# Layer 2 between images: the k, v and output projections by seven products of half-size blocks, with the block sums on VectorE

## Chip, cores and metric

The kernel runs on one core of one Trainium2 chip. The metric is device time in microseconds (us) of one execution, inputs laid out and output stored in the chip's memory. The core has five engines with an instruction queue each: TensorE (PE: matrix products, with a separate row PEld for loading the stationary operand), VectorE (DVE), ScalarE (ACT), GpSimd (POOL) and SyncE (SP, which here only issues transfers). Each executes its own queue in order; they meet at semaphores.

## The reference

Four layers on x of shape (4, 512, 32, 32) in float32: four images of 512 channels and 1024 tokens. Each layer normalizes x by groups of channels (`_gn`) and adds what it computes to x. Layer 0 is an attention with heads mixed, layer 1 a gate per channel, layer 3 a lookup of the eight best of 2048 memory rows. Layer 2 is what the change touches: a plain attention with 8 heads of 64 channels.

```python
def _L2_conv_ref(x, Wq, bq, Wkv, bkv, Wp, bp):        # x: _gn(x), shape (b, 512, 32, 32)
    q = _conv1x1(x, Wq, bq)
    k, v = jnp.split(_conv1x1(x, Wkv, bkv), 2, axis=1)
    ...                                               # to (b, 8, 64, 1024)
    attn = jax.nn.softmax(jnp.einsum('bhct,bhcs->bhts', q, k) * SCALE, axis=-1)
    out = jnp.einsum('bhts,bhcs->bhct', attn, v)
    return _conv1x1(out.reshape(b, c, h, w), Wp, bp)  # _conv1x1: 512 x 512 weights times 512 x 1024
x = x + _L2_conv_ref(_gn(x), ...)
```

Each of the four projections of an image is a product of a 512 x 512 matrix with a 512 x 1024 one.

## The kernel before

Everything is float32. Channels lie on the 128 partitions, in `KC` = 4 chunks; tokens run along the free dimension, cut in two halves of `NB` = 512. [...]

Layer 2 works on the images one after the other (`for b in range(B)`). For image b, 16 units of attention come first (`scores2`, `apply2`): four score tiles per unit, their exponentials on ScalarE, sums of pairs of exponentials on GpSimd and VectorE, and the products with v. Then, for b = 0, 1 and 2, comes the stretch between images, on TensorE in this order: `take_q2` (q of image b+1), the last `apply2` of b, `take_k2` with the denominators' product `rs` of b in it (`invert2`), `take_v2`, the first four score tiles of b+1, and `put_out2` (output projection of b). The last image is followed by `put_out2` alone. q, k and the output go through `project` (L192), v through `project_tokens` (L204); a projection is 32 products of 128 x 128 with 128 x 512, in four groups of eight, and each group fills a PSUM tile of two banks, `sc`, of which the pool `ps_s` has three. The score tiles and the small products of the normalizations (`small_ps`) take tiles of the same pool. A group is evacuated at once: q on VectorE (L989), k on ScalarE with its bias (L996), v on VectorE with its bias (L1005), and the output as two additions of 512 columns on VectorE (L1136) to a row block `xr_c` that ScalarE has scaled (L1134), followed by `bn_stats` (L1138).

`invert2` takes the denominators on a way through memory: `rs` on TensorE, a copy on ScalarE (L1099), a reciprocal on VectorE (L1100), a store `r` and a load `rb` by SP (L1106, L1109). `finish2` (L1121, VectorE) multiplies with `rb` and writes the attention's result `o`.

Beside the units run two chains of small steps as Python generators: `behind` (normalization for layer 3, `norm3`, and the gate of layer 1 for the last images, `gating`) and `ahead` (`prepare2`: normalized input `xn` of the next image). The loop takes a step of `behind` twice in each unit from the third on. All inner instructions keep the order in which they are written (`pin`); what isn't pinned is placed by the scheduler. Weights are loaded anew for each image into three rotating buffers (`eight_k`). The memory matrix of layer 3, `memT`, is loaded before layer 2 begins.

Of the kernel before, what the change touches and what calls it, by code (L numbers as in the profile page):

```python
# [10 lines left out]
F32 = mybir.dt.float32  # L11
AF = mybir.ActivationFunctionType
ALU = mybir.AluOpType
# [3 lines left out]
P = 128  # L17
B = 4
C = 512
T = 1024  # L20
KC = C // P
TC = T // P
NB = 512
# [6 lines left out]
NI = 2048  # L30
# [11 lines left out]
def fast_net(ctx: ExitStack, tc: tile.TileContext, a: dict, out: bass.AP, flag: bass.AP):  # L42
    nc = tc.nc
# [12 lines left out]
    def pin(ins):  # L56

        return tc.keep_in_program_order(ins)
# [182 lines left out]
    def big(tag, name):  # L241

        return apool.tile([P, KC, T], F32, tag=tag, name=name)
# [43 lines left out]
    def run_out(gen):  # L287
        for _ in gen:
            pass
# [662 lines left out]
    def prepare2(b, in_steps=False):  # L952

        I = img[b]
        mv2, s1, t1 = l2[b]
        if not in_steps:
            yield
        gm, rstd, _ = yield from coeffs(mv2[:, 0, :], mv2[:, 1, :], f"c{b}")
        sa = small.tile([P, KC], F32, tag="sa", name=f"sa_{b}")
        ta = small.tile([P, KC], F32, tag="ta", name=f"ta_{b}")  # L960
        nc.gpsimd.tensor_mul(sa, s1, rstd)
        nc.gpsimd.tensor_sub(ta, t1, gm)
        nc.gpsimd.tensor_mul(ta, ta, rstd)
        tb = I["tb"] = small.tile([P, KC], F32, tag="tb", name=f"tb_{b}")
        nc.gpsimd.tensor_add(tb, t1, bp2)
        if in_steps:
            yield from normalized(b, sa, ta)
            return
        xn = I["xn"] = big("xn", f"xn_c{b}")
        for k in range(KC):  # L970
            nc.sync.dma_start(out=xn[:, k, :], in_=x1[b][:, k, :])
        yield
        yield
        for k in range(KC):
            pin(nc.vector.tensor_scalar(
                xn[:, k, :], xn[:, k, :], sa[:, k:k + 1], ta[:, k:k + 1],
                ALU.mult, ALU.add,
            ))
            yield

    def load2(b):
        for key in ("Wq", "Wk", "Wv"):
            img[b][key] = load_w(key, f"{key}2_{b}")

    def take_q2(b, m, at=None):
        I = img[b]
        if m == 0:
            I["q"] = big("q", f"q2_{b}")
        project(I["Wq"], tokens(I["xn"]), m, at, lambda ps: pin(nc.vector.tensor_scalar(  # L989
            I["q"][:, m, :], ps, bq2[:, m:m + 1], SCALE, ALU.add, ALU.mult)), f"q2_{b}")  # L990

    def take_k2(b, m, at=None):
        I = img[b]
        if m == 0:
            I["k"] = big("k", f"k2_{b}")
        project(I["Wk"], tokens(I["xn"]), m, at, lambda ps: pin(nc.scalar.activation(  # L996
            I["k"][:, m, :], ps, AF.Identity, bias=bk2[:, m:m + 1])), f"k2_{b}")

    def take_v2(b, i, at=None):
        I = img[b]  # L1000
        if i == 0:
            I["v"] = big("v", f"v2_{b}").rearrange("p k (i c) -> p (k i) c", c=C)
        project_tokens(
            I["Wv"], lambda k, t: I["xn"][:, k, t * P:(t + 1) * P], i, at,
            lambda ps: pin(nc.vector.tensor_add(  # L1005
                I["v"][:, 2 * i:2 * i + 2, :], ps,
                bv2.rearrange("p c -> p () c").to_broadcast([P, 2, C]))), f"v2_{b}")
# [148 lines left out]
    def prepare3(b):  # L1156
        xn = xn3[b] = (o_full.rearrange("p (k t) -> p k t", k=KC) if b % 2
                       else big("xn", f"xn_d{b}"))
        gc3 = l3[b][1]
        for k in range(KC):  # L1160
            nc.sync.dma_start(out=xn[:, k, :], in_=x2[b][:, k, :])
        yield
        for k in range(KC):
            pin(nc.scalar.activation(
                xn[:, k, :], xn[:, k, :], AF.Identity,
                bias=gc3[:, 0, k:k + 1], scale=gc3[:, 1, k:k + 1],
            ))
            yield

    def attention(b, tt, between=None):  # L1170

        nm = f"{b}_{tt}"
        att = eight_k([P, NI], f"att_{nm}")
        for i, (lo, hi) in enumerate(
                ((0, T), (T, T + NB), (T + NB, NI)) if (b, tt) == tiles[-1] else ((0, T), (T, NI))):
            sc = ps_s.tile([P, T], F32, tag="sc", name=f"at_{nm}_{i}")
            for i0 in range(lo, hi, NB):
                for k in range(KC):
                    pin(nc.tensor.matmul(  # L1179
                        sc[:, i0 - lo:i0 - lo + NB],  # L1180
                        xn3[b][:, k, tt * P:(tt + 1) * P], memT[k][:, i0:i0 + NB],
                        start=(k == 0), stop=(k == KC - 1),
                    ))
# [261 lines left out]
    sums2 = eT_flat[:, 6 * 2 * NB:8 * 2 * NB].rearrange("p (i r q) -> p i r q", i=2, r=2)  # L1445
    pair_sum = e.rearrange("p i r qq k -> p i r (qq k)")
    memT = []
    for k in range(KC):
        if k < 2:
            m_ = apool.tile([P, NI], F32, tag="s2", bufs=2, name=f"memT{k}")  # L1450
        else:
            m_ = eT_flat[:, (4 + k) * NI:(5 + k) * NI]
        nc.sync.dma_start(out=m_, in_=a["memT"][k * P:(k + 1) * P, :])
        memT.append(m_)
# [4 lines left out]
    for b in range(B):  # L1459
        last = b + 1 == B  # L1460
        behind = chain(
            behind if b else state["behind"], norm3(b - 1) if b > 0 else gating(B - 1))
        ahead = prepare3(0) if last else prepare2(b + 1)
        for s, u in enumerate(UNITS2):
            if s == 5 and not last:
                load2(b + 1)
            if s == 5 and last:
                img[b]["Wp"] = load_w("Wp", f"Wp2_{b}")
            if s >= 1:
                scores2(b, u, UNITS2[s - 1])  # L1470
            for _ in range(2):
                if s >= 3:
# [4 lines left out]
        if not last:  # L1477
            for m in range(KC):
                take_q2(b + 1, m)
            img[b]["Wp"] = load_w("Wp", f"Wp2_{b}")  # L1480
        apply2(b, UNITS2[-1])
        if not last:
            for m in range(KC):
                take_k2(b + 1, m)
                if m == 0:
                    invert2(b)
        if last:
            atts[0] = attention(*tiles[0], lambda: invert2(b))
        finish2(b)
        if not last:  # L1490
            for i in range(TC // 2):
                take_v2(b + 1, i)
            scores2(b + 1, UNITS2[0])
        put_out2(b)

    def check_range():

# [751 lines left out]
```

## Time and profile before

| | |
|---|---|
| median of 3 runs | 2588.38 us (2588.32 to 2590.48) |
| the profiled execution's own time | 2587.3 us |
| its span, first to last instruction | 2585.5 us |
| TensorE clock granted over the span | 0.999 |
| busy share: PE, PEld, DVE, ACT, POOL | 98%, 45%, 60%, 38%, 46% |
| layer 2's stretch after image 0 on the chain that ended last | 1392.48 (q) to 1510.59 (end of the output projection) us |

The profile comes from one execution. Its page gives the busy time of each engine, the span in 40 slices, the chain of work that ended last (followed back from the last instruction), and groups of instructions by line, with busy time, the mean duration of one and the idle time of the engine ahead of them. Records of TensorE overlap, so its cost per record is the time of a run of records divided by their number, not the mean duration. Lines such as L192 are those of the kernel before.

### The profile page before, as it was taken

What the parts mean: (1) busy time and instruction counts of PE and PEld (TensorE: products, weight loads), DVE (VectorE), ACT (ScalarE), POOL (GpSimd) and SP (SyncE); (2) the same over time, 40 slices, a digit from 0 to 9 for tenths busy, and PEclk for the clock granted to TensorE, in tenths of its full rate; (3) what the DMA queues carried; (4) which work ended last, traced back from release to release, by engine and by line L of the source; (5) the groups of instructions that cost most, each with busy time, mean ns of one, the idle gap of its engine ahead of it and who ended that gap; (6) DMA issues with size and microseconds to landing.
All of it is one profiled execution on the core that took longest, in us unless ns stands there. A gap on an engine that the chain in (4) does not pass through costs nothing.

```text
span 2585.5 us, 47491 instructions
## 1 busy us (share of the span) xinstructions
PE 2533.4 (98%) x18438; PEld 1162.9 (45%) x18438; DVE 1548.0 (60%) x2668; ACT 986.9 (38%) x1165; POOL 1199.9 (46%) x1700
## 2 busy tenths in 40 slices
PE   8999999999999999999999999999999999999998
PEld 3344535544355534555533433443343344444445
DVE  4599348872788338881466047225614647878876
ACT  1467236651666236651252145125304622121211
POOL 3266415543455425553284047017404616656565
PEclk9999999999999999999999999999999999999999
DMA  2578448872698439883300120030012036667666
GB/s 82 144 208 233 124 125 228 232 205 82 180 239 235 113 95 224 236 254 122 130 18 15 68 101 21 25 137 27 13 42 97 22 110 184 216 185 219 180 192 180
DMA packets 186969, 358.22 MB, mean 139 GB/s; under 512 B 32873, under 2 KB 96361, under 8 KB 183026
## 3 DMA queue, kind: packets, MB, share of 16 engines
q1 hardware_dynamic: 105504, 175.57, 21.9%
q0 software_dynamic: 49152, 142.79, 20.1%
q10 hardware_dynamic: 32082, 36.76, 5.1%
q8 instruction: 148, 2.42, 0.4%
q14 instruction: 83, 0.68, 0.1%
HBM read 186.96 MB, written 33.82 MB: 85 GB/s over the span
## 4 chain that ended last, share of the span: by engine, by line
PE 74%; issue 8%; POOL 7%; DMA 7%; ACT 2%; DVE 1%; SPq 0%; POOLq 0%; ACTq 0%; DVEq 0%
PE pair L192 10%; PE sc_c L1027 9%; PE pv_c L1064 9%; PE pv L532 8%; POOL got L1204 7%; PE pair L467 6%; PE pair L493 5%; PE pt L425 4%; PE pt L721 4%; PE p L192 3%; PE k L192 3%; PE q L192 3%; PE v L204 3%; DMA got<-in_mem,ix 3%; DMA s<-ss 3%
## 5 line engine op out<-in xcount | busy, mean ns | idle before, releaser
L482 POOL DMA_DIRECT2D s<-ss x512 | 258.2, 511 | 399.1 <-ACT ss L473 103.3
L506 DVE STREAM_TRANSPOSE eT<-e 128x1024 f32<-128x1024 f32 x256 | 316.8, 1238 | 195.4 <-ACT e L500 194.9
L1204 POOL DMA_INDIRECT got<-in_mem,ix x256 | 277.6, 1085 | 216.2 <-DVE tmx L1210 144.3
L1021 ACT ACTIVATE eT<-sc_c 128x1024 f32<-128x1024 f32 x256 | 247.9, 1022 | 289.2 <-PE sc_c L1027 210.4
L521 DVE BATCH_NORM_STATS2 st<-e 128x6 f32<-128x256 f32 x1024 | 351.1, 406 | 0.0
L500 ACT ACTIVATE e<-pair 128x1024 f32<-128x1024 f32 x256 | 250.4, 1022 | 168.7 <-PE pair L493 139.0
L1045 POOL TENSOR_TENSOR e<-eT 128x1024 f32<-128x1024 f32 x96 | 235.6, 2457 | 161.6 <-ACT eT L1021 100.5
L467 PE MATMUL pair<-k,q 64*32 64x512 f32 x4096 | 267.1, 598 | 12.7 <-ACT e L500 12.7
L473 ACT COPY ss<-pair 128x1024 f32<-128x1024 f32 x256 | 247.2, 1020 | 78.6 <-PE pair L467 37.5
L532 PE MATMUL pv<-eT,v 128*64 128x128 f32 x4096 | 250.7, 276 | 8.9 <-ACT pv L592 8.9
L532 PEld LDWEIGHTS pv<-eT,v 128*64 128x64 f32 x4096 | 221.1, 137 | 76.7 <-issue 54.5
L1046 DVE TENSOR_TENSOR eT<-eT,e 128x1024 f32<-128x1024 f32 x96 | 138.7, 1444 | 179.0 <-POOL e L1045 178.9
L1027 PE MATMUL sc_c<-q,k 64*128 64x512 f32 x1024 | 237.2, 602 | 2.4 <-DVE xr L684 2.3
L1064 PE MATMUL pv_c<-eT,v 128*64 128x512 f32 x1024 | 234.7, 601 | 1.6 <-DVE eT L1121 1.6
L1041 POOL TENSOR_TENSOR eT<-eT 128x1024 f32<-128x1024 f32 x32 | 80.0, 2500 | 335.8 <-ACT eT L1021 332.0
L493 PE MATMUL pair<-s,wmix 32*32 32x512 f32 x4096 | 161.8, 599 | 3.1 <-DMA s<-ss 1.9
L1251 DVE SCALAR_TENSOR_TENSOR acc<-got,et,acc 128x512 f32<-128x512 f32 x210 | 157.9, 752 | 7.5
L1027 PEld LDWEIGHTS sc_c<-q,k 64*128 64x128 f32 x1024 | 93.5, 186 | 131.7 <-issue 72.0
L1184 ACT COPY att<-at 128x1024 f32<-128x1024 f32 (+1 forms) x65 | 64.9, 999 | 220.9 <-PE at L1179 220.8
L467 PEld LDWEIGHTS pair<-k,q 64*32 64x32 f32 x4096 | 57.1, 105 | 179.6 <-ACT e L500 86.3
L1064 PEld LDWEIGHTS pv_c<-eT,v 128*64 128x64 f32 x1024 | 68.4, 138 | 139.9 <-issue 138.1
L1179 PE MATMUL at<-memT,xn_d 128*128 128x512 f32 x256 | 120.7, 594 | 0.0
(295 smaller groups left out, 3299.4 us busy)
## 6 DMA issues: line engine op xcount, KB each, us to landing
s<-ss SPq DMA_DIRECT2D x512, 128.0 KB
s<-ss POOLq DMA_DIRECT2D x512, 128.0 KB, 4.6
rb<-r POOLq DMA_DIRECT2D x64, 128.0 KB, 6.1
o<-o SPq DMA_DIRECT2D x32, 256.0 KB
xr<-in_x ACTq DMA_DIRECT2D x32, 256.0 KB
x<-xr SPq DMA_DIRECT2D x32, 256.0 KB
xr_c<-x SPq DMA_DIRECT2D x32, 256.0 KB
rb_c<-r SPq DMA_DIRECT2D x64, 128.0 KB
```

What stands on the lines that cost most here:

```text
L192: pin(nc.tensor.matmul(ps[:, n, :], w[:, k, m * P:(m + 1) * P], rhs(k, n), start=(k == 0), stop=(k == KC - 1),))
L467: pin(nc.tensor.matmul(sc[m * NS:(m + 1) * NS, r, :], q[r * HD:(r + 1) * HD, m, s * NS:(s + 1) * NS], k_[r * HD:(r + 1) * HD, m, n * NB:(n ...
L482: pin(relays[side].dma_start(out=s2[2 * m + r::NH], in_=ss[m * NS:(m + 1) * NS, r, :]))
L493: pin(nc.tensor.matmul(mixed(s, r // 2)[t * NS:(t + 1) * NS, r % 2, :].rearrange("p (qq k) -> p qq k", qq=2), wmix[r * NS:(r + 1) * NS], s ...
L500: pin(nc.scalar.activation(e[:, half].rearrange("p r qq k -> p (r qq k)"), flat2(mixed(s, half)), AF.Exp))
L506: pin(nc.vector.transpose(eT[:, j % 2].rearrange("p b (qq i r) x -> p i r qq b x", qq=2, i=4)[:, i, 2 * half:2 * half + 2], e[:, half].rea ...
L521: pin(nc.vector.bn_stats(st[:, i, 2 * half + r, qq, :], e[:, half, r, qq, :]))
L532: pin(nc.tensor.matmul(pv[r * HD:(r + 1) * HD, gp, :], I["v"][:, t, g * HD:(g + 1) * HD], eT[:, j % 2, t, :, 4 * g:4 * g + 4], start=(t == ...
L1021: pin(nc.scalar.activation(e, scs[len(es)], AF.Exp))
L1027: pin(nc.tensor.matmul(sc[:, r, :], I["k"][r * HD:(r + 1) * HD, m, t * P:(t + 1) * P], I["q"][r * HD:(r + 1) * HD, m, n * NB:(n + 1) * NB] ...
L1064: pin(nc.tensor.matmul(pv[r * HD:(r + 1) * HD, :], I["v"][:, t, h * HD:(h + 1) * HD], e[:, r, :], start=(t == 0), stop=(t == TC - 1),))
L1204: pin(nc.gpsimd.indirect_dma_start(out=got[:, i, :], out_offset=None, in_=a["mem"], in_offset=bass.IndirectOffsetOnAxis(ap=ix[:, i:i + 1], ...
```

## The change

For b = 0, 1 and 2 the k, v and output projections are computed by seven products of half-size blocks (256 x 256 blocks of the weights with 256 x 512 blocks of the input) in place of eight. Each of the seven is four products of 128 x 128 with 128 x 512 (k and output, `by_channels`) or eight of 128 x 128 with 128 x 256 (v, `by_tokens`), accumulated in pairs, and takes one `sc` tile. The sums of blocks that the products need are made on VectorE: of the input in `input_sums` (five additions of 128 x 1024 for k and v together, five for the output), of each weight matrix once, in `weight_sums` (five additions of 128 x 512, between image 0 and 1); the summed weights are stored to memory (`w_sums`) and loaded in place of the plain ones afterwards. Each of the seven results goes into one or two of the four blocks of the projection: the first use of a block is written by `begin` (ScalarE for k and output, VectorE for v), the others are added or subtracted in place by VectorE. The output's blocks are finished by `done`: a `scalar_tensor_tensor` with the row block, `bn_stats`, and a store of the whole block.

It also moves things. The steps of `behind` leave the units (but for the last image) and are taken between the groups of q, the products of k and those of v. `memT` is loaded at the beginning of the last image, since the block sums lie in its place. The last image keeps `put_out2`.

```diff
     def load2(b):
         for key in ("Wq", "Wk", "Wv"):
-            img[b][key] = load_w(key, f"{key}2_{b}")
+            load_sums(b, key, b == 1 or key == "Wq")
...
+    def input_sums(src):
+        b11, b12, b21, b22 = quarters(src, NB)
+        t1, t3, t4 = places7["in"]
+        return ((lambda: add7(t1, b11, b22), lambda: sub7(t4, b21, b11), lambda: sub7(t3, b12, b22)),
+                (lambda: add7(b21, b21, b22), lambda: add7(b12, b11, b12)))
...
+    SEVEN = (
+        (1, ((0, 0, "="), (1, 1, "="))),
+        (4, ((0, 0, "+"), (1, 0, "="))),
+        (3, ((0, 1, "="), (1, 1, "+"))),
+        (5, ((0, 0, "-"), (0, 1, "+"))),
+        (2, ((1, 0, "+"), (1, 1, "-"))),
+        (7, ((0, 0, "+"),)),
+        (6, ((1, 1, "+"),)),
+    )
+    LAST7 = {3: (5, (0, 1)), 4: (2, (1, 0)), 5: (7, (0, 0)), 6: (6, (1, 1))}
...
+    def seven(b, key, src, multiply, view, block, begin, done=None):
...
+        for i, (at, uses) in enumerate(SEVEN):
+            ps = ps_s.tile([P, 2, NB], F32, tag="sc", name=f"{key}_{b}_{at}")
+            multiply(ps, *factors[at])
+            for *ij, op in uses:
+                if op == "=":
+                    begin(*ij, ps)
+                else:
+                    (add7 if op == "+" else sub7)(block(*ij), block(*ij), view(ps))
+            if done and i in LAST7:
+                done(*LAST7[i][1])
+            yield
+
+    def by_channels(ps, w, x):
+        for m in range(2):
+            for k in range(2):
+                pin(nc.tensor.matmul(
+                    ps[:, m, :], w[:, k, m * P:(m + 1) * P], x[:, k, :],
+                    start=(k == 0), stop=(k == 1)))
+
+    def by_tokens(ps, w, x):
+        for t in range(4):
+            for k in range(2):
+                pin(nc.tensor.matmul(
+                    by_head(ps)[:, t, :], x[:, k, t * P:(t + 1) * P], w[:, k, :],
+                    start=(k == 0), stop=(k == 1)))
...
+        def done(i, j):
+            for m in range(2 * i, 2 * i + 2):
+                part = dst[:, m, j * NB:(j + 1) * NB]
+                pin(nc.vector.scalar_tensor_tensor(
+                    part, rows.pop((m, j)), s1[:, m:m + 1], part, ALU.mult, ALU.add))
+                pin(nc.vector.bn_stats(st[m][:, j, :], part))
...
-            for m in range(KC):
-                take_k2(b + 1, m)
-                if m == 0:
-                    invert2(b)
+        for i, _ in enumerate(seven_k(b + 1)):
+            if i == 0:
+                invert2(b)
+                for fn in later:
+                    fn()
+            if i == 4 and b == 0:
+                weight_sums(0, "Wp")
+            next(behind, None)
         finish2(b)
...
-            for i in range(TC // 2):
-                take_v2(b + 1, i)
-            scores2(b + 1, UNITS2[0])
-        put_out2(b)
+        early, later = input_sums(img[b]["o"])
+        for i, _ in enumerate(seven_v(b + 1)):
+            if 2 <= i < 5:
+                early[i - 2]()
+            elif i >= 5:
+                later[i - 5]()
+            next(behind, None)
+        run_out(behind)
+        scores2(b + 1, UNITS2[0])
+        seven_out(b)
```

More of the change, by code (lines that the diff above doesn't have):

```diff
@@ L982, in load2, with load_sums @@
         for key in ("Wq", "Wk", "Wv"):
-            img[b][key] = load_w(key, f"{key}2_{b}")
+            load_sums(b, key, b == 1 or key == "Wq")
+    def load_sums(b, key, plain):
+        w = img[b][key] = eight_k([P, KC, C], f"{key}2_{b}")
+        nc.sync.dma_start(out=w, in_=a[key] if plain else w_sums[key])
+    H = C // 2
+    w_sums = {key: dram.tile([P, KC, C], F32, tag=f"ws_{key}", name=f"ws_{key}")
+              for key in ("Wk", "Wv", "Wp")}
+    places7 = {}
+    add7, sub7 = (lambda *t: pin(nc.vector.tensor_add(*t))), (lambda *t: pin(nc.vector.tensor_sub(*t)))
@@ new lines, in quarters, with weight_sums @@
+    def quarters(t, step):
+        return [t[:, 2 * h:2 * h + 2, i * step:(i + 1) * step]
+                for h in range(2) for i in range(2)]
+    def input_sums(src):
[3 more added lines that the diff above has]
+                (lambda: add7(b21, b21, b22), lambda: add7(b12, b11, b12)))
+    def weight_sums(b, key):
+        w = img[b][key]
+        a11, a21, a12, a22 = quarters(w, H)
+        s1, s6, s7 = places7[key]
+        add7(s1, a11, a22)
+        sub7(s7, a12, a22)
+        add7(a12, a11, a12)
+        sub7(s6, a21, a11)
+        add7(a21, a21, a22)
+        nc.sync.dma_start(out=w_sums[key], in_=w)
@@ new lines, in fast_net, with by_head @@
+    SEVEN = (
[8 more added lines that the diff above has]
+    LAST7 = {3: (5, (0, 1)), 4: (2, (1, 0)), 5: (7, (0, 0)), 6: (6, (1, 1))}
+    def by_head(ps):
+        return ps.rearrange("p n (t c) -> p (n t) c", c=H)
+    def seven(b, key, src, multiply, view, block, begin, done=None):
+        a11, s2, s5, a22 = quarters(img[b][key], H)
+        s1, s6, s7 = places7[key]
+        b11, t6, t7, b22 = quarters(src, NB)
+        t1, t3, t4 = places7["in"]
+        factors = {1: (s1, t1), 2: (s2, b11), 3: (a11, t3), 4: (a22, t4),
+                   5: (s5, b22), 6: (s6, t6), 7: (s7, t7)}
+        for i, (at, uses) in enumerate(SEVEN):
[9 more added lines that the diff above has]
+            yield
@@ new lines, in seven_k, with begin, seven_v, block @@
+    def seven_k(b):
+        dst = img[b]["k"] = big("k", f"k2_{b}")
+        def begin(i, j, ps):
+            for m in range(2 * i, 2 * i + 2):
+                pin(nc.scalar.activation(
+                    dst[:, m, j * NB:(j + 1) * NB], ps[:, m % 2, :],
+                    AF.Identity, bias=bk2[:, m:m + 1]))
+        return seven(b, "Wk", img[b]["xn"], by_channels, lambda ps: ps,
+                     lambda i, j: dst[:, 2 * i:2 * i + 2, j * NB:(j + 1) * NB], begin)
+    def seven_v(b):
+        dst = img[b]["v"] = big("v", f"v2_{b}").rearrange("p k (i c) -> p (k i) c", c=C)
+        def block(i, j):
+            return dst[:, 4 * j:4 * j + 4, i * H:(i + 1) * H]
+        def begin(i, j, ps):
+            pin(nc.vector.tensor_add(
+                block(i, j), by_head(ps),
+                bv2[:, i * H:(i + 1) * H].rearrange("p c -> p () c").to_broadcast([P, 4, H])))
+        return seven(b, "Wv", img[b]["xn"], by_tokens, by_head, block, begin)
@@ new lines, in seven_out, with load, block, begin @@
+    def seven_out(b):
+        I = img[b]
+        s1 = l2[b][1]
+        dst = big("xn", f"out_{b}")
+        mv = small.tile([P, KC, 2], F32, tag="mv", name=f"mv_d{b}")
+        st = [small.tile([P, 2, 6], F32, tag="bnst", name=f"st_d{b}_{m}") for m in range(KC)]
+        order = [LAST7[i][1] for i in sorted(LAST7)]
+        rows = {}
+        def load(at):
+            i, j = order[at]
+            for r in range(2):
+                m = 2 * i + r
+                tag, bufs = (("xr", 2), (("o1", "xs")[r], 1))[at % 2]
+                x_ = rows[m, j] = apool.tile(
+                    [P, NB], F32, tag=tag, bufs=bufs, name=f"xr_c{b}_{m}_{j}")
+                nc.sync.dma_start(out=x_, in_=x1[b][:, m, j * NB:(j + 1) * NB])
+        def block(i, j):
+            return dst[:, 2 * i:2 * i + 2, j * NB:(j + 1) * NB]
+        def begin(i, j, ps):
+            for m in range(2 * i, 2 * i + 2):
+                pin(nc.scalar.activation(
+                    dst[:, m, j * NB:(j + 1) * NB], ps[:, m % 2, :],
+                    AF.Identity, bias=I["tb"][:, m:m + 1]))
+        def done(i, j):
+            for m in range(2 * i, 2 * i + 2):
+                part = dst[:, m, j * NB:(j + 1) * NB]
+                pin(nc.vector.scalar_tensor_tensor(
+                    part, rows.pop((m, j)), s1[:, m:m + 1], part, ALU.mult, ALU.add))
+                pin(nc.vector.bn_stats(st[m][:, j, :], part))
+                if (i, j) in ((0, 0), (1, 1)):
+                    pin(nc.vector.bn_aggr(mv[:, m, :], st[m].rearrange("p i s -> p (i s)")))
+            nc.sync.dma_start(
+                out=x2[b][:, 2 * i:2 * i + 2, j * NB:(j + 1) * NB], in_=block(i, j))
+            at = order.index((i, j)) + 2
+            if at < len(order):
+                load(at)
+        load(0)
+        load(1)
+        run_out(seven(b, "Wp", I["o"], by_channels, lambda ps: ps, block, begin, done))
+        l3[b] = (mv, const.tile([P, 2, KC], F32, tag=f"gc3_{b}", name=f"gc3_{b}"))
@@ L1447, in fast_net, with load_memory @@
     memT = []
[L1448 to L1454, printed above, removed]
+    def load_memory():
+        for k in range(KC):
+            if k < 2:
+                m_ = apool.tile([P, NI], F32, tag="s2", bufs=2, name=f"memT{k}")
+            else:
+                m_ = eT_flat[:, (4 + k) * NI:(5 + k) * NI]
+            nc.sync.dma_start(out=m_, in_=a["memT"][k * P:(k + 1) * P, :])
+            memT.append(m_)
+    two7 = [apool.tile([P, 2, 2, NB], F32, tag="s2", bufs=2, name=f"sums7_{i}") for i in range(2)]
+    places7["in"] = two7[0][:, 0], two7[0][:, 1], two7[1][:, 0]
+    nine = [eT_flat[:, 6 * NI + i * C:6 * NI + (i + 1) * C].rearrange("p (k c) -> p k c", k=2)
+            for i in range(8)] + [two7[1][:, 1, 0].rearrange("p (k c) -> p k c", k=2)]
+    for i, key in enumerate(("Wk", "Wv", "Wp")):
+        places7[key] = nine[3 * i:3 * i + 3]
     nc.gpsimd.tensor_scalar_mul(same, same, 8.0 / T)
@@ L1463, in fast_net @@
         ahead = prepare3(0) if last else prepare2(b + 1)
+        if last:
+            load_memory()
         for s, u in enumerate(UNITS2):
@@ L1471, in fast_net @@
             for _ in range(2):
-                if s >= 3:
+                if s >= 3 and last:
                     next(behind, None)
@@ L1476, in fast_net @@
         run_out(ahead)
-        if not last:
-            for m in range(KC):
-                take_q2(b + 1, m)
-            img[b]["Wp"] = load_w("Wp", f"Wp2_{b}")
-        apply2(b, UNITS2[-1])
-        if not last:
-            for m in range(KC):
-                take_k2(b + 1, m)
-                if m == 0:
-                    invert2(b)
-        if last:
-            atts[0] = attention(*tiles[0], lambda: invert2(b))
-        finish2(b)
-        if not last:
-            for i in range(TC // 2):
-                take_v2(b + 1, i)
-            scores2(b + 1, UNITS2[0])
-        put_out2(b)
+        if last:
+            apply2(b, UNITS2[-1])
+            atts[0] = attention(*tiles[0], lambda: invert2(b))
+            finish2(b)
+            put_out2(b)
+            continue
+        early, later = input_sums(img[b + 1]["xn"])
+        for m in range(KC):
+            take_q2(b + 1, m)
+            if m < 3:
+                early[m]()
+            if b == 0 and m < 2:
+                weight_sums(1, ("Wk", "Wv")[m])
+            next(behind, None)
+        load_sums(b, "Wp", b == 0)
+        apply2(b, UNITS2[-1])
+        for i, _ in enumerate(seven_k(b + 1)):
[6 more added lines that the diff above has]
+            next(behind, None)
+        finish2(b)
+        early, later = input_sums(img[b]["o"])
[4 more added lines that the diff above has]
+                later[i - 5]()
+            next(behind, None)
+        run_out(behind)
+        scores2(b + 1, UNITS2[0])
+        seven_out(b)
     def check_range():
```

## The prediction

> **What bounds the kernel now.** I read the engines' busy shares first, then the chain that ended last in order of time, then a table of the stretch between image 0 and image 1 by stage.
>
> ```profile
> PE 2533.4 (98%) x18438; PEld 1162.9 (45%) x18438; DVE 1548.0 (60%) x2668; ACT 986.9 (38%) x1165; POOL 1199.9 (46%) x1700
> ```
>
> TensorE is busy nearly always; 98% could still hide waits, since ends of records are modelled. The chain of layer 2 settles it (start, duration, what):
>
> ```profile
> 1392.48 27.66 PE q L192 x64
> 1420.14 3.58 PE pv_c L1064 x16
> 1423.73 7.06 PE k L192 x16
> 1431.03 20.80 PE k L192 x48
> 1451.83 27.47 PE v L204 x64
> 1479.29 3.63 PE sc_c L1027 x16
> 1482.93 27.66 PE p L192 x64
> 1510.59 3.63 PE sc_c L1027 x16
> ```
>
> Here every piece is TensorE and each begins where the last ended. A projection is 64 records (two for each product in the program) in 27.66 us: 0.432 us for a record of 512 columns. The windows of q, k, v and output (us, then busy time of PE, PEld, DVE, ACT, POOL, clock, DMA share, GB/s):
>
> ```profile
> 1395.00:1420.00 25.00, 25.00 (x59) 10.83 (x57) 11.86 (x14) 0.00 (x0) 1.99 (x1) 1.00 0.03 11
> 1424.00:1451.00 27.00, 27.00 (x67) 11.89 (x66) 1.52 (x5) 3.41 (x4) 0.00 (x0) 1.00 0.05 14
> 1452.00:1479.00 27.00, 27.00 (x64) 11.78 (x62) 3.67 (x3) 0.98 (x1) 0.00 (x0) 1.00 0.11 39
> 1483.00:1510.00 27.00, 27.00 (x63) 11.93 (x64) 9.34 (x16) 5.93 (x9) 4.13 (x2) 1.00 0.56 202
> ```
>
> PE is full, and VectorE is all but free in just these stages: 1.5, 3.7 and 9.3 us of 27. So a record less is time less, and VectorE has room, though how much is the question. The groups I cost with (busy, mean of one, idle ahead):
>
> ```profile
> L745 PE MATMUL pair<-eT 128*128 128x256 f32 x128 | 27.8, 379 | 0.0
> L1046 DVE TENSOR_TENSOR eT<-eT,e 128x1024 f32<-128x1024 f32 x96 | 138.7, 1444 | 179.0 <-POOL e L1045 178.9
> L1251 DVE SCALAR_TENSOR_TENSOR acc<-got,et,acc 128x512 f32<-128x512 f32 x210 | 157.9, 752 | 7.5
> L1005 DVE TENSOR_TENSOR v<-v,bv 128x1024 f32<-128x1024 f32 x12 | 14.7, 1225 | 112.1 <-PE v L204 112.1
> L996 ACT ACTIVATE k<-k,bk 128x1024 f32<-128x1024 f32 x12 | 13.4, 1113 | 169.5 <-PE k L192 169.5
> L592 ACT COPY pv<-pv 128x512 f32<-128x512 f32 x32 | 19.0, 593 | 36.3 <-POOL ampt L879 21.5 <-PE pv L532 14.8
> L1138 DVE BATCH_NORM_STATS2 st_d<-xr_c 128x6 f32<-128x512 f32 x32 | 20.4, 680 | 0.0
> ```
>
> **Removed on the path: TensorE records.** k and output: 7 products x 8 records = 56 in place of 64, at the same shape: 8 x 0.432 = 3.46 us each. v: 7 x 16 = 112 records of 256 columns. Their price is L745's, back to back with a new stationary operand each: 27.8/128 = 0.217 us, so 112 x 0.217 = 24.3 for 27.5, 3.2 less. The far row is L721, 384 records of the same shape strewn among other work, 95.7/384 = 0.249: then v costs 27.9, and nothing is won there. I take L745, which is a solid projection as v is. An image gives 3.46 + 3.2 + 3.46 = 10.1 us, three images 30.3.
>
> [...] L745 already has loads of 0.190 and a pace of 0.217, so the measurement decides for full overlap.
>
> **Added off the path: VectorE.** An addition of 1024 columns from PSUM is L1005's 1.225. One from SBUF is L1046: median 1.225, mean 1.444 because of some that met GpSimd's additions, worst 3.39; GpSimd is idle in these windows but for 1.99 and 4.13 us, so I take 1.225, with 1.444 as the upper end. No row shows anything cheaper for two tensors, so the lower end is 1.21, the least of L1046.
> - q (27.7 us): 4 evacuations of 1.28 and 3 sums, 8.8 us; after image 0 also ten sums of 512 columns at some 0.69 (L1136), 15.7. Hidden.
> - k (24.2): 6 additions in the first five products, 2 behind, 2 input sums, some 1.7 for the denominators and `finish2`, about 14, and 3.4 for Wp's sums once. Hidden.
> - v (24.3): 4 biased copies, 8 additions in place and 5 sums for the output: 17 x 1.225 = 20.8. It fits. Walked product by product (3.48 each; VectorE 2.45, 2.45, 3.7, 3.7, 3.7, 2.45, 2.45), VectorE ends 2.5 us after TensorE, and no product finds its tile still taken.
> - output (24.2): 8 additions, 8 `scalar_tensor_tensor` of 0.75, 8 `bn_stats` of 0.68, 4 aggregates of 0.21: 9.8 + 6.0 + 5.4 + 0.8 = 22.1 us, but bunched at the end. This is where something is left over.
>
> **The output's tail.** Count from the stage's start; products end at 3.46, 6.91 ... 24.19. In the built order VectorE takes product 5's additions (13.9 to 16.4) and two finished rows (2 x 1.43, to 19.2), product 2's (21.7) and its rows (24.5), product 7's addition (25.8), rows with aggregates (29.0), product 6's addition (30.3). The scores that follow take the tiles in the built order thus: the first gets product 2's (free), the second product 7's. It could begin at 25.1 and waits until 25.9. The fourth then waits for the exponential of the second: four tiles end at 28.9 rather than 27.8, a loss of 1.1 us. Product 6's tile comes only a unit later, at 32.5, so 30.3 does no harm. If VectorE is 2 us later (a row block behind the 1 MB load of Wv on SP's queue, or a meeting with GpSimd), the loss is 3. Lower end: none. VectorE's backlog of some 9 us is worked off in the units, of which it uses 81 in 118 us (busy time from 1511 to 1629); the next denominators are wanted by PE 18 us after the output, and are ready at some 15 to 17.
>
> **Added waits.** `finish2` stands in VectorE's queue ahead of the third product's addition and waits for `rb`, 4.95 us after `r` is issued (1432.68 to 1437.63): about 12.3 us into k. Behind it wait the additions to products 3 and 5; the tile of product 3 is wanted at 17.5. Five us of cover; without it, that much per us. In image 0's stretch `rs` and a step of `gating` take two of three tiles, so the second product of k needs the first's tile back: four biased copies on ScalarE of 0.593 (L592) to 0.69 (L996 halved, with its fixed part) after it, 2.8 us, less 0.6 for the small products: 2.2 us lost, once. ScalarE and VectorE never read one tile at a time in the built order, a wait more per product (1.3 us), inside the three-tile cover.
>
> **Moved.** `behind`'s products stay on PE at the same number; their GpSimd steps have a product (3.46 us) each instead of half a unit (3.7), so no gain and no loss. On SP's queue the weight stores (3 x 1 MB, once) go ahead of Wp's load, which is wanted 17 us after its issue; `memT`, 4 MB, goes behind the last image's Wp and is wanted 16 units later. Summed weights replace plain ones byte for byte. DMA share there is 0.03 to 0.56, so nothing of it reaches PE.
>
> **Sum.** 30.3 - 2.2 - 3 x 1.1 = 24.8 us. On the profiled execution's own 2587.3 us that is 2562.5; the median, 1.1 above it, gives 2563.6.
>
> **Rivals.**
> - *The gain is halved by tiles or by v's records.* For it: L721's 0.249 (v's 3 x 3.6 = 10.7 us gone: 2574.3), or a tail of 4 us instead of 1.1 per image (8.7: 2572). Against: L745, and tiles in the built order. With both, 2583.
> - *VectorE becomes the bound: slower.* Place: v to output. With p the price of an addition, VectorE needs 25 p + 12.3 us (17 + 8 additions; the rows' 6.0 + 5.4 + 0.8) against 24.3 + 3.6 + 24.2 = 52.1 of TensorE (v, scores, output) plus some 5 of tile cover. It stalls PE from p = 1.8, eats the 10.1 us from p = 2.2, and at p = 2.5 costs 74.8 - 57.1 = 17.7 per image, 7.6 net: 2588.4 + 22.8 = 2611. For it: L1046's worst of 3.39 and TensorE's own writing to PSUM meanwhile. Against: L1005 read PSUM during products, and no PSUM addition is over 1.23.
> - *It changes nothing:* the number of records doesn't fall or PE waits exactly as much. Only if stalls come to 10 us an image; the built order has 56 and 112 records.
>
> **Numbers.** The forecast (2557 to 2570) has 0.62, the halved gain (2570 to 2583) 0.23, the slower case 0.10, no change 0.05. Range: from 2557 (no stalls, 30.3 off, and a little) to 2582, with the halved gain in it. A measurement can tell about 0.2%, 5.2 us, from no change: faster 0.85, same 0.05, slower 0.10.
>
> **What would show it.** Right: 56 records per k and output and 112 per v, stages of about 24.3 us; DVE at 1.23 per addition and over 80% busy in v and output; PE waiting on a VectorE addition of some 0.7 us at the second score tile after each output, and 2.2 us on ScalarE in k of image 1. Wrong: PE waits on DVE within v or the output, a pace over 0.23 in v, additions at 1.4 or more, or waits for `rb` that reach PE.

## The result, and the profile after

The changed kernel takes 2557.65 us (median of 6 runs, 2554.46 to 2561.19) against 2588.43 for the kernel before; the ratio is 0.9887, with a 95% interval of 0.9875 to 0.9898. The profiled execution took 2558.4 us with a span of 2556.6, 28.9 less than that of before. The forecast was 2563.6, the range 2557 to 2582.

The line of busy shares:

```profile
PE 2503.3 (98%) x18534; PEld 1180.8 (46%) x18534; DVE 1685.8 (66%) x2785; ACT 985.8 (39%) x1177; POOL 1192.5 (47%) x1700
```

TensorE is busy for 30 us less at the same share, and has 96 records more: 144 more in v, which are half as wide, and 48 fewer in k and the output. VectorE takes on 138 us in the whole program. The chain of layer 2 between image 1 and 2, where nothing disturbs it:

```profile
1637.85 3.63 PE Wk L1056 x8
1641.48 0.24 PE rs L1251 x4
1641.72 20.80 PE Wk L1056 x48
1662.52 24.17 PE Wv L1063 x112
1686.69 3.63 PE sc_c L1183 x16
1690.32 13.95 PE Wp L1056 x32
...
1714.48 1.22 DVE out L993
1715.69 0.04 issue
1715.74 1.15 PE sc_c L1183 x4
```

56 records for k and 112 for v stand where 64 stood, each group without a gap: 24.4 and 24.2 us for 27.9 and 27.5. In the output the chain leaves TensorE for VectorE, where product 7's addition ends 1.2 us after TensorE's last product (1715.7 against 1690.25 + 24.2); the second score tile waits for that. The windows of q, k, v and output of this stretch (us, then busy time of PE, PEld, DVE, ACT, POOL, clock, DMA share, GB/s):

```profile
1606.10:1634.20 28.10, 28.10 (x71) 12.51 (x69) 14.30 (x17) 0.32 (x2) 5.56 (x9) 1.00 0.08 28
1637.80:1662.30 24.50, 24.50 (x62) 10.84 (x61) 12.06 (x14) 4.92 (x9) 0.00 (x0) 1.00 0.19 65
1662.40:1686.60 24.20, 24.20 (x113) 21.04 (x111) 18.65 (x16) 0.00 (x0) 0.00 (x0) 1.00 0.14 45
1690.30:1714.50 24.20, 24.20 (x60) 10.53 (x58) 13.70 (x16) 6.27 (x10) 4.23 (x2) 1.00 0.23 73
```

PE is still full in all four; VectorE's busy time in k, v and output went from 1.5, 3.7 and 9.3 us to 12.1, 18.7 and 13.7. The groups that carry it (busy, mean ns of one, idle ahead):

```profile
L1063 PE MATMUL Wv<-Wv,sums 128*128 128x256 f32 x96 | 21.5, 380 | 0.0
L1063 PEld LDWEIGHTS Wv<-Wv,sums 128*128 128x128 f32 x96 | 18.2, 190 | 2.5
L993 DVE TENSOR_TENSOR v<-v,Wv 128x1024 f32<-128x1024 f32 x24 | 28.7, 1218 | 7.8 <-PE Wv L1063 7.8
L1125 DVE SCALAR_TENSOR_TENSOR out<-xr_c,s,out 128x512 f32<-128x512 f32 x24 | 21.4, 891 | 0.2
```

An addition costs 1.22 us, v's pace is 24.17 / 112 = 0.216 us. A row of the output costs 0.70 to 0.75 us, as costed, in 21 of 24 cases; the other three met GpSimd and took 1.96, which makes the mean 0.89.

Most of the rest of this document counts in **layer 2's time**: from the end of the last product at L745 to the first product with the memory matrix (`at`). It is 812.7 us before and 782.8 after, 30.0 less. What else differs between the two profiled runs the change does not touch: layers 0 and 1 were 3.3 us shorter and layer 3 4.3 us longer, and in a second profile of the same kernel (`after_again`) 0.9 longer and 0.0. Whole times therefore scatter by some us, and layer 2 is the better measure.

| layer 2, us | before | after | difference |
|---|---|---|---|
| k, three images | 28.0 each | 27.7, 24.6, 24.6 | 3 x 3.43 less; 2.0 more for a wait and 1.2 for small products in image 1 |
| v, three images | 27.6 each | 26.2, 24.3, 24.3 | 3 x 3.29 less; 1.9 more for small products in image 1 |
| output, three images | 27.7 each | 24.2 each | 3 x 3.43 less |
| first four score tiles after the output | 3.63, 4.04, 3.63 | 4.62 each | twice 0.99 more, once 0.58 |
| image 0's units, up to q | 124.0 | 117.2 | 6.8 less |

These add up to 30.5 - 2.0 - 3.1 - 2.6 + 6.8 = 29.6. The units of images 1 and 2 are, behind these tiles, 1.3 us shorter and q 0.9 longer, since the small products of `norm3` moved there: 30.0 in all.

The last row was not in the sum. The timeline of TensorE before, at the end of image 0's units, and VectorE's shortly ahead of it (the last bracket is idle time and its releaser):

```profile
1370.62 0.31 PE L1095 MATMUL rs<-s_c,same 128*64 128x32 f32 x4 [2.03 <-DVE s_c L1081]
1372.58 5.35 PE L1064 MATMUL pv_c<-eT,v 128*64 128x512 f32 x16 [1.64 <-DVE eT L1121]
```

```profile
1358.66 3.36 DVE L1046 TENSOR_TENSOR eT<-eT,e 128x1024 f32<-128x1024 f32 x1 [2.52 <-POOL e L1045]
1364.60 3.38 DVE L1046 TENSOR_TENSOR eT<-eT,e 128x1024 f32<-128x1024 f32 x1
```

TensorE waited 3.67 us for the denominators, whose pair sums were late: GpSimd had the small steps of `gating` between its own additions (two of them, of 1.18 and 1.08 us, between 1360 and 1370), and two of VectorE's additions took 3.4 us rather than 1.2. And behind the wait 16 records took 5.35 us, where they take 3.65 elsewhere: 1.7 more, at a granted clock of 0.83 in the window of 10 us:

```profile
1370.00:1380.00 10.00, 7.73 (x30) 2.76 (x32) 9.97 (x11) 3.14 (x4) 5.37 (x2) 0.83 0.00 0
```

### The profile page after: what moved, and what is told of

It is laid out like the page before. It is cut to its first block, busy times and chain, and to the rows that moved or that the text cites. A ratio compares the mean times of both kernels' runs of the same rounds, so it can differ in the third digit from the quotient of the medians.

```text
span 2556.6 us, 47828 instructions
## 1 busy us (share of the span) xinstructions
PE 2503.3 (98%) x18534; PEld 1180.8 (46%) x18534; DVE 1685.8 (66%) x2785; ACT 985.8 (39%) x1177; POOL 1192.5 (47%) x1700
## 4 chain that ended last, share of the span: by engine, by line
PE 74%; issue 10%; POOL 7%; DVE 3%; ACT 3%; DMA 2%; POOLq 0%; SPq 0%; ACTq 0%; DVEq 0%
PE pair L192 10%; PE sc_c L1183 9%; PE pv_c L1220 9%; PE pv L532 8%; POOL got L1360 7%; PE pair L467 6%; PE pair L493 5%; PE pt L425 5%; PE pt L721 4%; PE q L192 3%; PE Wk L1056 3%; PE Wv L1063 3%; ACT e L500 2%; PE Wp L1056 2%; PE at L1335 2%
## 5 line engine op out<-in xcount | busy, mean ns | idle before, releaser
L1202 DVE TENSOR_TENSOR eT<-eT,e 128x1024 f32<-128x1024 f32 x96 | 136.3, 1420 | 146.3 <-POOL e L1201 146.1
```

## Experiments

**The move of the small steps alone** (`moved_alone`): the kernel before, with

```diff
-                if s >= 3:
+                if s >= 3 and last:
                     next(behind, None)
...
                 take_q2(b + 1, m)
+                next(behind, None)
...
+                for _ in range(2 if m < 3 else 1):
+                    next(behind, None)
...
+                for _ in range(2 if i < 3 else 1):
+                    next(behind, None)
+            run_out(behind)
             scores2(b + 1, UNITS2[0])
```

> The kernel before with one part of the change alone: the steps of `behind` (normalization for layer 3, gate of layer 1) leave the units and run between the groups of q, k and v; all projections stay plain and memT is loaded where it was. Layer 2 is read from the end of its last preparing product (L745) to the first product with the memory matrix: 812.8 us in the kernel before, 782.8 after. The prediction's step (the move costs and gains nothing) expects 812.8 and 2588 us. The rival, read from the two traces: GpSimd's small steps delayed the pair sums of image 0's last units, for which TensorE waited 2.0 + 1.6 us, and a small product costs 0.31 us between score products and 0.14 between projections; it expects 3.7 us less, about 1 to 2 less for some twelve small products, and up to 1 back where the second group of k has to wait for the bank of the first: 808 to 809, and 2583 to 2585 us in all.

Layer 2 takes 807.6 us, 5.2 less, as the rival said and a little better; the wait of 3.67 and the slow 16 records are gone, and k's second group waits 0.6. These are all of TensorE's waits in layer 2 (the first is in the kernel before as well):

```profile
PE sc_c L1027 <- DVE xr L684: 2.3, 1, 2.3
PE k L192 <- ACT k L996: 0.6, 1, 0.6
```

In all it took 2583.26 us against 2584.88 for the kernel before, measured beside it; the ratio is 0.9994 (0.9984 to 1.0004). That is 1.6 us less, and by the interval between 4.1 less and 1.0 more. So the 5.2 is what one profile of each kernel shows, and more than an execution gains on average. 1.7 of it is the clock, which drops behind such a wait in some executions and not in others (see the end); the 3.5 left lie inside the interval. Whether the wait itself comes in every execution of the kernel before, its one profile does not show. By the traces the prediction's step "no gain and no loss" falls; the whole times alone would not refute it.

**v undone** (`v_plain`):

```diff
-            load_sums(b, key, b == 1 or key == "Wq")
+            load_sums(b, key, b == 1 or key != "Wk")
...
-        for i, _ in enumerate(seven_v(b + 1)):
...
+        for i in range(TC // 2):
+            take_v2(b + 1, i)
...
```

> The kernel after with v undone: v by 64 records of 512 columns with plain weights, k and output by seven products. (v of images 1 to 3 is computed from an input whose two outer blocks already hold sums, so its values differ; the work is that of a plain v.) The prediction's step, 112 records at 0.217 us hide their weight loads and a v saves 3.3 us, expects 3 x 3.3 = 9.9 us more: layer 2 792.7 us, about 2567.5 in all. If short records cost as where they lie strewn (0.249), v by seven saves nothing and this run is within 1 us of the kernel after. If VectorE's 17 additions in v held TensorE up anywhere, the loss is smaller than 9.9.

Layer 2 takes 790.95 us. In the profiled run of the kernel after, the clock dropped at the start of layer 2 and cost 1.7 us (see the end); here it did not. Without that the kernel after stands at 781.1, as `after_again` confirms, and the loss is 9.9, as expected. The three v take 29.5, 27.6 and 27.6 us for 26.2, 24.3 and 24.3. In all: 2567.95, ratio 0.9943 (0.9923 to 0.9963). VectorE's 17 additions held up nothing.

**The output undone** (`out_plain`):

```diff
-        load_sums(b, "Wp", b == 0)
+        img[b]["Wp"] = load_w("Wp", f"Wp2_{b}")
...
-        early, later = input_sums(img[b]["o"])
...
-        seven_out(b)
+        put_out2(b)
```

> The kernel after with the output undone: output projection by 64 records as in the kernel before, k and v by seven products, no sums of o and of Wp. By the prediction's steps, 8 records more cost 3.46 us an image and the wait of the second score tile (measured 1.05 us) goes: 3 x (3.46 - 1.05) = 7.2 us more, layer 2 790.0 us, about 2565 in all. If VectorE's backlog after the output costs something further back in the units, the loss is less than 7.2; if it costs nothing at all, 10.4.

Layer 2: 788.4 us, 7.3 more than 781.1. So the output's seven products bring 3.43 an image and its tail costs 1.0. In all 2565.83, ratio 0.9939 (0.9916 to 0.9961).

**Another order in the output** (`rows_later`):

```diff
-            if done and i in LAST7:
-                done(*LAST7[i][1])
+            if done and i == 3:
+                done(*LAST7[3][1])
+            if done and i in (5, 6):
+                done(*LAST7[i - 1][1])
             yield
+        if done:
+            done(*LAST7[6][1])
```

> The kernel after with VectorE's order in the output changed: the finished rows of product 2 come after product 7's addition, those of 7 and 6 after product 6's. By the prediction's walk product 7's addition then ends at 22.9 us of the stage, before the score tile that takes its bank begins (24.2), so the wait of 1.05 us after each output goes: 3.1 us less, layer 2 779.7 us. Rival: the work only moves on, the next tile or the next denominators are as late as before, and layer 2 stays at 782.8.

Layer 2: 791.3 us, 10.2 worse than 781.1. TensorE's waits in layer 2:

```profile
PE rs L1255 <- DVE s_c L1241: 6.0, 3, 2.0
PE sc_c L1187 <- DVE xr L684: 2.3, 1, 2.3
PE Wk L1060 <- ACT k L1077: 2.0, 1, 2.0
PE sc_c L1187 <- DVE out L993: 1.2, 3, 0.4
```

The four score tiles after the output lose 0.67 us in place of 0.99 (the third waits 0.4 for product 6's addition), and the denominators are 2.0 late three times: the rows that were put off ran into GpSimd's pair sums. VectorE in that place:

```profile
1727.88 0.70 DVE L1129 SCALAR_TENSOR_TENSOR out<-xr_c,s,out 128x512 f32<-128x512 f32 x1
1728.50 3.38 DVE L1206 TENSOR_TENSOR eT<-eT,e 128x1024 f32<-128x1024 f32 x1
...
1732.64 2.24 DVE L1129 SCALAR_TENSOR_TENSOR out<-xr_c,s,out 128x512 f32<-128x512 f32 x1
...
1735.77 3.22 DVE L1206 TENSOR_TENSOR eT<-eT,e 128x1024 f32<-128x1024 f32 x1
```

The same operations take 0.7 or 2.2, and 1.2 or 3.4 us. Both kinds have two operands in SBUF. In the trace of the kernel after, the 24 rows (L1125) and, from 1265 to 2040 us, 94 pair sums (L1202) divide by their start: the 3 rows and 9 pair sums that begin inside a GpSimd addition of 128 x 1024 took 1.96 to 1.97 and 3.22 to 3.40 us, of the others none took over 0.75 and 1.23. The slow ones here fit that: the excess, 1.5 and 2.2 us, is a little less than one such addition (2.35 to 2.37 us in the last section). What holds them up, no trace shows. The additions from PSUM (L993), with one operand in SBUF, keep their 1.2 beside GpSimd, as the last section shows. The expectation's walk was right for product 7's addition, which ends at 22.7 us of the stage, and looked neither at the tile after the next nor at the denominators. The clock dropped three times in this run, to 0.83 in the windows of 10 us from 1270, 1420 and 1960, some 1.7 us each, twice behind waits that the kernel after has as well: some 3.3 of the 10.2 us are not the new order's.

**One step later in k** (`step_later`):

```diff
-            next(behind, None)
+            if i or b:
+                next(behind, None)
```

> The kernel after with one step moved: between image 0 and 1 the first step of `gating` comes after the second product of k, not after the first. By the prediction's step (the second product needs the bank of the first, since rs and the step hold the other two) the second product now takes a free bank and the wait of 2.0 us in k of image 1 goes: layer 2 780.8 us, or 779.1 if the clock does not drop at its start as it did in the profiled run of the kernel after (782.8 with a drop of 1.7). Rival: the step takes the bank of the first product one product later and the wait only moves: 782.8 or 781.1.

This run, the next two and the first of `rows_first` are one execution each. k of image 1 takes 25.2 us for 27.7, the wait is gone and does not come back. Layer 2 as a whole took 784.7, because two other things happened in this run: the drop at the start, and in image 2's units, which the edit does not touch, this:

```profile
1716.80 2.71 DVE L1125 SCALAR_TENSOR_TENSOR out<-xr_c,s,out 128x512 f32<-128x512 f32 x1 [0.82 <-DMA xr_c<-x]
1734.55 0.31 PE L1251 MATMUL rs<-s_c,same 128*64 128x32 f32 x4 [2.00 <-DVE s_c L1237]
1734.65 5.36 PE L1220 MATMUL pv_c<-eT,v 128*64 128x512 f32 x16
```

A row block landed 0.8 us late, the row took 2.71 us for 0.75, the denominators were 2.0 late, and behind the wait the clock dropped to 0.81 in the window from 1732 to 1738: nearly 4 us for 0.8. In the kernel after the sums end at 1731.9 and are wanted at 1733.6: a margin of 1.7 us.

**More work for VectorE** (`extra_1`, and `extra_3` with three in place of one):

```diff
+            if key != "Wk":
+                for _ in range(1):
+                    add7(places7["spare"], bv2, bv2)
```

> The kernel after with 14 more VectorE additions of 512 columns (0.68 us each) an image, one behind the additions of each product of v and of the output; their result is not used. That is 9.6 us more, as if each of the 25 additions took 1.22 + 0.38 = 1.60 us. By the prediction's rival (VectorE needs 25 p + 12.3 us against 57.1) TensorE is held up from p = 1.8: nothing in v or the output, layer 2 781 to 783 us. Rival, from the last run but one: what VectorE still owes after the output delays the pair sums and so the denominators of the next image, and TensorE waits some 2 us or more an image for them, though v and the output still fit: 787 to 812.

> The kernel after with 42 more VectorE additions of 512 columns an image, three behind each product of v and of the output (28.7 us, as if an addition took 2.37 us). By the prediction's rival VectorE needs 25 x 2.37 + 12.3 = 71.6 us against 57.1 and TensorE loses 14.5 us an image: layer 2 782.8 + 43 = 826 us, more than the kernel before (812.7). If the units take up part of the arrears, less: 800 to 820.

With one per product the additions took 0.68 us each (median), with three 0.69, but 11 of those 126 took 1.2 to 2.8. One per product: 785.7 us, 4.7 more, with no wait inside v or the output: 1.1 an image come at the four score tiles after the output, and 0.7 at the four between v and the output of images 2 and 3; the denominators were in time. It lies between the two theories: TensorE begins to lose before p = 1.8, since the work is bunched where a stage ends. Three per product: 831.8 us, 50.7 more than 781.1. Of this 3.2 is the clock, which dropped at the start of layer 2 (0.91 and 0.92 in the two windows of 10 us from 1260) and in k of image 1 (0.83 from 1420 to 1430); the rest is 14.7, 16.4 and 16.4 us for the three images, where the formula has 14.5 (19.8 with the 34.0 us an image that the added work in fact took, for 28.7). In each of these three the clock dropped twice more (0.83 in five windows of 10 us, 0.94 and 0.89 in two that adjoin); at the 1.7 us that a drop cost above, some 3.4 us of each are the clock, an estimate. So the prediction's slower rival was a real mechanism, and its price the right size, but not its place: 7.7 us of each image's loss lie behind the output. The waits show where:

```profile
PE sc_c L1186 <- ACT eT L1180: 10.6, 9, 1.2
PE sc_c L1186 <- DVE out L993: 10.2, 6, 3.1
PE Wp L1059 <- DVE v L993: 7.4, 3, 2.5
PE sc_c L1186 <- DVE v L993: 4.3, 4, 1.4
```

**The rows first** (`rows_first`): the row blocks of x go into the output's place, ScalarE scales them there, and VectorE only adds.

```diff
+    def take_row(b, m, j):
+        part = img[b + 1]["xn"][:, m, j * NB:(j + 1) * NB]
+        nc.sync.dma_start(out=part, in_=x1[b][:, m, j * NB:(j + 1) * NB])
+        pin(nc.scalar.activation(
+            part, part, AF.Identity, bias=img[b]["tb"][:, m:m + 1], scale=l2[b][1][:, m:m + 1]))
...
         def begin(i, j, ps):
-            for m in range(2 * i, 2 * i + 2):
...
+            add7(block(i, j), block(i, j), ps)
...
-                pin(nc.vector.scalar_tensor_tensor(
-                    part, rows.pop((m, j)), s1[:, m:m + 1], part, ALU.mult, ALU.add))
```

> The kernel after with the output's rows taken first: the row blocks of x are loaded into the place of the output (which is xn's, free block by block as v's products read it), scaled and biased there by ScalarE, and all twelve uses of the seven products are additions in place. VectorE loses 8 scalar_tensor_tensor (6.0 us) near the end and gains 4 additions (4.9 us) near the start of the output. By the walk of the prediction product 7's addition ends at 22.7 us of the stage and product 6's rows at 27.5, not 33.5: the wait of 1.05 us an image goes, 3.1 us less, layer 2 779.7 us (778.0 without a drop of the clock). Rival: the rows land late (1 MB of them can only be loaded when v is done) and TensorE waits for a bank in the output, some 2 to 4 us an image: 786 to 792.

Layer 2: 778.1 us, as expected to 0.1. TensorE after the output:

```profile
1710.03 3.60 PE L1056 MATMUL Wp<-eT 128*128 128x512 f32 x8
1713.56 3.70 PE L1171 MATMUL sc_c<-q,k 64*128 64x512 f32 x16
1717.19 3.65 PE L1208 MATMUL pv_c<-eT,v 128*64 128x512 f32 x16
```

No gap is left. The denominators' sums end at 1726.5 and are wanted at 1731.6, a margin of 5 us for 1.7.

**Timed together**: the kernel after, the rows first, and a version with q by seven products as well.

> The kernel after once more, beside the next two. Layer 2 781.1 us without a drop of the clock, 1.7 more for each drop behind a wait; a wait of 2.0 us for the denominators in some image's first units, as in the run with the moved step, is possible, since the sums they need end only 1.6 us ahead of their use. In all 2554 to 2561 us as in its six runs so far.

> The kernel with the rows taken first, once more and timed: layer 2 778.1 us as in its one run, 3 us less than the kernel after without a drop of the clock. Since its denominators are ready 5 us ahead of their use, its runs should show no wait there; 2549 to 2553 us in all, a ratio of about 0.987 to the kernel before.

> Rows first and the first step of `gating` one product later, and q of images 1 to 3 by seven products too: its weight sums are made in image 0's units (stored, and loaded again for each image), the five sums of the input in the last units ahead of q, and SCALE goes into the exponentials. A q saves 3.46 us as a k does: 778.1 - 2.0 - 3 x 3.46 = 765.7 us for layer 2, about 2539 in all. Rival: the five input sums (6.1 us of VectorE in the units) and the weight sums delay the pair sums; the denominators come too late in the last units, and TensorE waits 2 us or more an image, with a drop of the clock of 1.7 behind some: 772 to 777, 2546 to 2550 in all.

| | layer 2, us | median, us | ratio to before (95%) |
|---|---|---|---|
| after_again | 781.1 | 2556.93 | 0.9891 (0.9872 to 0.9909) |
| rows_first_again | 778.1 | 2554.55 | 0.9876 (0.9858 to 0.9894) |
| all_three | 780.2 | 2553.63 | 0.9879 (0.9862 to 0.9895) |

Rows first is 3.0 us better than the kernel after in layer 2, in both of its profiles; the whole times differ by 2.4, which their intervals do not separate. `all_three` is worse than either of its expectations. q by seven products saved 3.3 us in image 1 and 2.3 in the others, and gave it back in the units:

```profile
1382.52 0.43 PE L1259 MATMUL rs<-s_c,same 128*64 128x32 f32 x4 [5.12 <-DVE s_c L1245]
1384.16 6.45 PE L1228 MATMUL pv_c<-eT,v 128*64 128x512 f32 x16 [1.21 <-DVE eT L1285]
```

Image 0's units took 125.4 us for 115.5. The sums of q's weights and input stood in VectorE's queue ahead of the pair sums.

**q of two images, with fewer sums in the units** (`q_of_two`):

> Rows first, the first step of the small chains one product later, and q by seven products for images 2 and 3 alone: the sums of Wq are made beside the plain q of image 1 and stored, two of the five sums of an input (2.4 us of VectorE) stay in the last two units ahead of q, the other three and no small steps run in q, and SCALE goes into the exponentials of images 2 and 3. If what spoilt the last try was only VectorE's work in the units (waits of 5.1 and 3.3 us, a clock of 0.51 behind them) and the small products between q's, this gives 778.1 - 2.0 - 2 x 3.46 = 769.2 us for layer 2. Rival: also two sums in the units cost 1 us an image and the small products' banks 2 us in k: 772 to 775.

Layer 2: 784.8 us, in all 2560.83, ratio 0.9902 (0.9886 to 0.9919): worse than without q, and again worse than both expectations. In image 2, and alike in image 3, the second product of q waits for its input sum, and its records are slow behind the wait (16 in 9.51 us, where they take 7.0 in the output of the kernel after; the clock was 0.66 in the window from 1610 to 1620):

```profile
1614.21 9.51 PE L1063 MATMUL Wq<-sums,Wq 128*128 128x512 f32 x16 [5.41 <-issue]
```

The row names no releaser. On VectorE's timeline the sum that the product reads ends at 1614.1:

```profile
1605.19 3.35 DVE L1217 TENSOR_TENSOR eT<-eT,e 128x1024 f32<-128x1024 f32 x1 [2.26 <-POOL e L1216]
...
1612.90 2.35 DVE L1000 TENSOR_TENSOR sums<-xn_c 128x1024 f32<-128x1024 f32 x2
```

It was queued behind a pair sum that waits for GpSimd, and behind the denominators. Neither try with q beats the rows first in layer 2 (`all_three` is 0.9 us lower in whole time, which the intervals do not separate); an order that puts q's products without input sums first was not tried.

## Why the prediction was right, and where not

- *Records are time.* Right to 0.1 us: 3.43 for 3.46 (k, output) and 3.29 for 3.2 (v). `v_plain` and `out_plain` give the same by undoing. That the weight loads hide at 0.216 us a record is shown: a load takes 0.190 us in v (L1063), and 112 records with a load each took 24.2 us without a gap.
- *An addition costs 1.225.* Right: 1.22 and 1.21 in all three stages.
- *VectorE in v ends 2.5 us after TensorE and no tile is late.* Right: 2.5 (1689.08 against 1686.62), no wait.
- *The output's tail costs 1.1 an image.* Right: 0.99. VectorE's walk holds nearly to the tenth: product 5's additions 14.0 to 16.4 us of the stage, product 7's ends at 25.4, the fourth tile at 28.9. Only the row that met GpSimd, behind these tiles, cost more (1.96 for 0.75).
- *2.2 us in k of image 1 for a bank.* Right: 2.0, released by ScalarE; `step_later` takes it away.
- *VectorE over 80% busy in v and output.* This sign did not come: 77% and 57% (18.65 and 13.70 of 24.20 us). It did not follow from the prediction's own walk, in which VectorE's work ends 2.5 us behind v and some 9 behind the output.
- *`finish2` waits for `rb` without reaching TensorE.* Right: VectorE waits 1.2 us, TensorE not.
- *The denominators are ready 15 to 17 us after the output and wanted at 18.* Nearly: 17.4 and 19.1. The margin of 1.7 us is thin, and what follows when it is used up, as in `rows_later`, was not in the range's working.
- *`behind` moves without gain or loss.* This step failed, and it is the term of the sum that was mis-sized: 0 where the profile of `moved_alone` has 5.2 us less in layer 2 (3.67 of waiting and 1.7 of clock gone) and its whole time 1.6 less (4.1 less to 1.0 more). I looked at the steps' place among the products and at GpSimd in the stretch, and not at image 0's units, where GpSimd was 80% busy (87.6 of 110 us from 1270 to 1380; 78.8 in `moved_alone`) and TensorE waited already.

With that term as the profiles have it the sum is 24.8 + 5.2 = 30.0. That layer 2 shows 30.0 too is chance: the kernel after lost 1.7 us to a clock drop at its start that the profile of the kernel before does not have, and without it the difference is 31.7. Of the 1.7 left, 0.6 is the wait in k, which `moved_alone` has and the sum counts already, 0.7 is the tail (2.6 in all for 3.3), and the rest a tenth or two in k's wait and in the records.

The median lies 0.65 us inside the lower end of the range, 6 below the forecast. There is luck in that: the end at 2557 was put for a kernel without stalls. The stalls came as forecast, and a term that stood at nothing made up for them. Whole times put the gain at 30.8 us in the first measurement and at 27.8 beside `after_again` (2584.68 to 2556.93), for a forecast of 24.8.

Of the rivals, the halved gain falls with 0.216 and 1.0, "changes nothing" with the records. The slower one is a true mechanism, but its threshold of 1.8 us is too high (at 1.6 TensorE loses 1.6 us an image), and at 2.37 its 14.5 us an image came as 14.7 to 16.4, about half of it behind the output; as the added work also took longer than was put in, and the clock dropped in each image, the closeness is in part chance.

## What to carry over

Where one engine was full and its neighbour had room, a record less was its time less (3.43 us for eight), and the terms of the sum could be had to a few tenths of a us by walking the neighbour's queue product by product. Walk it past the end of the stage as well, up to the next thing that the full engine wants from it: that was the thin place here. And before a step is called free where it goes, read the waits of the stage it leaves, not only of the one it goes to.

## What the runs showed of the hardware

**A short wait can cost twice.** Windows of 5 us at the start of layer 2 in the kernel after, behind a wait of 2.3 us:

```profile
1265.00:1270.00 5.00, 2.68 (x8) 1.20 (x9) 3.24 (x7) 0.54 (x1) 0.00 (x0) 0.77 0.51 168
1270.00:1275.00 5.00, 5.00 (x24) 2.51 (x22) 0.00 (x0) 4.37 (x6) 2.78 (x2) 0.89 0.24 76
```

The granted clock is 0.77 and 0.89, and 32 records take 8.83 us. Behind the same wait of 2.3 us in `v_plain` they take 7.14 at full clock. Of the 14 profiles here four had the drop at this place. Behind the wait of 2.0 us in k of image 1 two of nine had it, and behind denominators 2.0 late two of four. Each of these cost 1.55 to 1.71 us. Behind a longer wait the drop is plainer: in `all_three`, around waits of 5.1 and 1.2 us, the clock was 0.51 in the window from 1380 to 1390.

So waits of 2.0 and 2.3 us could be enough for a drop, and such a wait cost between 2.0 and 4.0 us. Why the clock drops behind some of them and not behind others, no trace shows. Part of the scatter between runs of one kernel may be this: of the 13 runs of the kernel before that were measured beside `moved_alone`, the fastest took 2579.5 us at a mean granted clock of 1.000, the slowest 2593.9 at 0.997.

**VectorE beside GpSimd** cost nothing for an addition that reads PSUM (of the 72 in k, v and output of the kernel after none took over 1.22 us, and the three that lie inside a GpSimd addition of 128 x 1024 took 1.17), and up to 2.2 us for an operation with two operands in SBUF (3.40 for 1.22, a pair sum). GpSimd and VectorE behind the output of the kernel after, from their timelines:

```profile
1718.07 2.37 POOL L1201 TENSOR_TENSOR e<-eT 128x1024 f32<-128x1024 f32 x1 [23.54 <-DVE out L1125]
1722.31 2.35 POOL L1201 TENSOR_TENSOR e<-eT 128x1024 f32<-128x1024 f32 x1 [1.87 <-ACT eT L1177]
```

```profile
1718.95 1.17 DVE L993 TENSOR_TENSOR out<-out,Wp 128x1024 f32<-128x1024 f32 x1
...
1723.25 1.96 DVE L1125 SCALAR_TENSOR_TENSOR out<-xr_c,s,out 128x512 f32<-128x512 f32 x1
```

The addition from PSUM lies inside the first GpSimd addition and takes 1.17; the row begins inside the second and ends 0.55 us after it, nearly as if it had begun only then. In k and v of this image GpSimd was idle (0.00 in the windows above); it is the tail of the output where the two meet.
